# Attention layer of a graph network on one core: outputs' products and last channels' sums split by pair of chunks, and a new order of a step

## Chip, cores and metric

The kernel runs on one NeuronCore of a Trainium2 chip. The metric is the device time of one execution in microseconds. Several executions are timed, and one more is profiled; the profiled one has a time of its own.

## What is computed

Four graph layers work one after the other on 6250 nodes of 160 numbers (64 scalars and 32 vectors of three components) with 100,000 edges sorted by their target node. Each is followed by a residual sum and a layer norm. The change lies in the first, the attention layer. Cut to what matters:

```python
msg_s = (s_n @ Ws_src)[src] + (s_n @ Ws_dst)[dst]          # gathered per edge; vectors likewise
w1 = rbf @ W_rbf
m1_s, m1_v = _cg_tp(msg_s, msg_v, y0, y1, ...w1...)          # tensor product with the edge's direction
a = leaky(m1_s @ W_alpha); a = sum(a * alpha_dot)            # one score per head and edge
alpha = softmax of a over the edges of one target node
val_s, val_v = m1_s @ Ws_val, m1_v @ Wv_val, gated by sigmoid
m2_s, m2_v = _cg_tp(val_s, val_v, y0, y1, ...)
h = [m2_s @ Ws_vlin, m2_v @ Wv_vlin]
agg = segment_sum(alpha * h, dst)
out = node + [agg_s @ Wps, agg_v @ Wpv]
```

## The kernel before, in words

**Tiling.** Edges are cut into 784 chunks of 128. Four chunks (WC0) make a window, and 196 windows make the layer (`NST`, L1639). Class `Window0` (L1247) holds one window, and each of its methods is one stage of the work on it. Two chunks of a window make a pair `p`; each chunk sums into 16 target nodes of its own.

**Stages.** A window goes through these, in order of the data:
- `edges` (L1270, four calls) and `nodes` (L1276) gather rows from DRAM by an indirect DMA that GpSimd (POOL) issues, through the helper `gather` (L786, trace line L787).
- `masks`, `ends`, `weights` (TensorE, L1297 and L1302), `features` (DVE, L1308), `dots` (DVE, L1331), `dot` (GpSimd, L1335, two calls) and `product1` (DVE, four calls) make the first tensor product.
- For each chunk: `turn` (TensorE, three transposes, L1345), `turned` (ScalarE or ACT, L1350), `linear` (TensorE, three products, L1357), `tanh` (ACT, L1362), `directed` (DVE, L1372 to L1374).
- `crossed` (DVE, L1380), `joined` (GpSimd, L1386 and L1388), `gates`, `values` and `gated` make the values.
- `channels` (TensorE, L1415), `leak` and `leaky`, `scores` (TensorE, L1428), `largest` (DVE, L1437), `negated`, `exps`, `denominators` and `by_edge` (TensorE, L1466) make the attention weights. `weighted` (DVE, L1473) multiplies them with the edge's direction into the tile `py`.
- `sums` (TensorE, L1481, one call for each pair) sums values over the edges. `sums_z` (L1488, products at L1493) does it for the last 32 channels, 16 small products for all four chunks. `summed` and `summed_z` (ACT, L1486 and L1500) copy the sums out of PSUM.
- `outputs` (L1502, products at L1512) multiplies the sums with the outputs' weights: 40 small products, 20 for each pair, into one PSUM tile. `even` (ACT, L1517) and `odd` (DVE, L1521) take them out, and `write` sends the rows to DRAM by SyncE (SP).

Every float32 product is two rows of the trace (two passes), with as many weight loads.

**What sets the order.** Nothing is scheduled by the tool here: `edge_loop0` (L1601) runs under a manual schedule. A table written out by hand, `STEP0` (L1586), lists (lag, stage, argument). In step `s` the loop at L1661 goes down the table and calls each stage on window `s - lag`. So eight windows are in work at once (lags 0 to 7), and each engine's instructions stand in its queue in the order of this table. [...]

**Buffers.** PSUM tiles named `m` come from a ring of four banks (`bank`, L1337): each new one waits until the one four before it has been read. Fifteen are taken in a step. `wf` takes the other four banks. `py`, `a`, `az`, `q`, `th`, `xt` and the two `tp` tiles alternate between two buffers, `f` between five, `fw` between four.

**Every fourth step** (`k == 0`) the loads and the multiplication of the radial inputs take place: `radial_load` and `ends_load` on SP, `radial_turn` (GpSimd, L1570).

Behind the loop stands a slow path for edges that fit no window (L1668 on). It runs `todo_a` times and calls the same stages by name for one pair.

In the order before, TensorE's part of one step is: turns of two chunks, by_edge, ends, weights, turns of two chunks, scores, sums of pair 0, sums_z (16), linear of two chunks, sums of pair 1, linear of two chunks, channels, outputs (40). GpSimd's part is: dot 1, dot 2, nodes, edges 2, (radial_turn,) edges 0, edges 3, joined 0, edges 1, joined 1.

Of the kernel before, what the change touches and what calls it, by code (L numbers as in the profile page):

```python
# [18 lines left out]
P = 128  # L19
# [3 lines left out]
S, V = 64, 32  # L23
F = S + 3 * V
# [23 lines left out]
def kernel(ctx: ExitStack, tc: tile.TileContext, t: dict, out: bass.AP):  # L48
    nc = tc.nc
    vec, act, pe, pool = nc.vector, nc.scalar, nc.tensor, nc.gpsimd  # L50
# [151 lines left out]
    with tc.tile_pool(name="win", bufs=1) as sb, tc.tile_pool(name="winp", bufs=1, space=PSUM) as ps:  # L202
# [20 lines left out]
        for h in range(2):  # L223
            q = slice(h * WN, (h + 1) * WN)
# [7 lines left out]
        a = sb.tile([P, NCH], F32, name="a")  # L232
# [113 lines left out]
        for g, c in enumerate(ORDER0):  # L346
            q = slice(32 * g, 32 * g + 32)
# [4 lines left out]
        for h in range(2):  # L352
            q = slice(S * h, S * h + S)
# [893 lines left out]
    class Window0:  # L1247
# [12 lines left out]
        def __init__(self, w, sb, ps, n, k, radial, dst, gi, y, yc, ids, node_idx, rows, tps):  # L1260
            self.w, self.sb, self.ps, self.n, self.np = w, sb, ps, n, n // 2
            self.k, self.radial, self.dst = k, radial, dst
            self.gi, self.y, self.yc, self.ids, self.node_idx = gi, y, yc, ids, node_idx
            self.rows, self.tps = rows, tps
            self.t, self.z, self.pa = {}, {}, {}
            self.f = self.xt = self.th = self.q = self.val = self.a = None

            self.groups = [(g, c) for g, c in enumerate(ORDER0) if c < n]

# [215 lines left out]
                self.a = self.sb.tile([P, WC0, 4, S], F32, name="a", bufs=2)  # L1485
            act.copy(self.a[:, 2 * p : 2 * p + 2].rearrange("p c i m -> p (c i m)"), self.pa[p])  # L1486

        def sums_z(self):  # L1488

            self.pz = pa = self.bank()  # L1490
            for c in range(self.n):
                for i in range(4):
                    pe.matmul(  # L1493
                        pa[i * V : (i + 1) * V, c * S : (c + 1) * S], self.val[:, c, P:F], self.py[:, c, i, :], start=True, stop=True
                    )

        def summed_z(self):
# [1 line left out]
            self.az = self.sb.tile([P, WC0, S], F32, name="az", bufs=2)  # L1499
            act.copy(self.az[:, 0:n].rearrange("p c m -> p (c m)"), self.pz[:, 0 : n * S])  # L1500

        def outputs(self):  # L1502

            w = self.w["o"]
            self.po = po = self.bank()[:, 0:160].rearrange("p (a k) -> p a k", a=2)
            for p in range(self.np):
                for i in range(5):
                    for h in range(2):
                        for g in range(2):
                            q = slice(h * S + g * 32, h * S + g * 32 + 32)  # L1510
                            x = (self.a[:, 2 * p + h, i, :] if i < 4 else self.az[:, 2 * p + h, :])[:, g * 32 : g * 32 + 32]
                            pe.matmul(po[q, p, :], x, w[:, i, g, :], start=i == 0, stop=i == 4)  # L1512

        def even(self):

# [56 lines left out]
    class Ends:  # L1572
# [11 lines left out]


    STEP0 = [  # L1586
        (7, "summed", 1), (4, "linear", 1), (0, "radial_load"), (4, "tanh", 1), (4, "linear", 3), (1, "edges", 0),
        (5, "negated"), (3, "product1", 2), (4, "channels"), (1, "edges", 3), (4, "tanh", 3), (6, "denominators"),
        (4, "leak"), (4, "directed", 1), (5, "exps"), (7, "outputs"), (3, "turn", 3), (4, "directed", 3),
        (4, "leaky"), (5, "values"), (7, "even"), (3, "turn", 2), (4, "others"), (5, "by_edge"), (4, "crossed"),  # L1590
        (7, "odd"), (5, "gates"), (2, "ends"), (5, "weighted"), (4, "joined", 0), (3, "turned", 3),
        (3, "turned", 2), (2, "weights"), (3, "turn", 0), (3, "turned", 0), (3, "turn", 1), (2, "features"),
        (1, "edges", 1), (4, "scores"), (3, "bases"), (2, "dots"), (4, "largest"), (3, "turned", 1), (6, "sums", 0),
        (6, "summed", 0), (6, "sums_z"), (0, "ends_load"), (7, "write", 0), (3, "linear", 0), (5, "joined", 1),
        (3, "linear", 2), (6, "sums", 1), (2, "product1", 0), (2, "dot", 1), (2, "dot", 2), (1, "masks"),
        (3, "tanh", 0), (2, "product1", 1), (7, "write", 2), (7, "write", 1), (6, "summed_z"), (5, "gated"),
        (3, "tanh", 2), (0, "nodes"), (3, "directed", 0), (3, "directed", 2), (1, "edges", 2), (2, "product1", 3),
        (7, "write", 3), (0, "radial_turn"),
    ]

    def edge_loop0(w, res):  # L1601
        with tc.tile_pool(name="sb0", bufs=1) as sb, tc.tile_pool(name="ps0", bufs=1, space=PSUM) as ps:
# [37 lines left out]
            with tc.manual_schedule():  # L1640
                for s in range(NST + max(x[0] for x in STEP0)):
                    if s < NST:
# [10 lines left out]
                        q = slice(c0, c0 + WC0)  # L1653
# [13 lines left out]
        with ExitStack() as c2:  # L1667
            n_it = nc.values_load(todo_a[0:1, 0:1], min_val=0, max_val=NIT)  # L1668
            it = c2.enter_context(tc.For_i(0, n_it, 1))
            io = c2.enter_context(tc.tile_pool(name="late_0", bufs=1))  # L1670
            rows = ds(it * P, P)
            si = io.tile([P, CH], I32, name="si")
            nc.sync.dma_start(si, t["src_col"][rows, :])
            y5 = io.tile([P, CH, 5], F32, name="y5")
            nc.sync.dma_start(y5, t["ea5"][rows, :].rearrange("p (c i) -> p c i", i=5))

            y = io.tile([P, CH, 2, 6], F32, name="y")
            for h in range(2):
                vec.tensor_copy(y[:, :, h, 0:5], y5)
                vec.tensor_copy(y[:, :, h, 5:6], y5[:, :, 2:3])  # L1680
            at_ = io.tile([P, 1], F32, name="at0")
            vec.memset(at_, 0.0)
            c2.enter_context(tc.For_i(0, NP // (2 * WM0), 1))
            sb = c2.enter_context(tc.tile_pool(name="lsb0", bufs=1))
            ps = c2.enter_context(tc.tile_pool(name="lps0", bufs=1, space=PSUM))
            ids = sb.tile([P, 1], F32, name="ids")
            vec.tensor_scalar(ids, at_, slot0[:, 0:1], None, ALU.add)
            gi = sb.tile([P, 1], I32, name="gi")
            vec.tensor_copy(gi, ids)
            gh = sb.tile([P, 1], I32, name="gh")  # L1690
            vec.tensor_scalar(gh, at_, slot0[:, 1:2], None, ALU.add)
            vec.tensor_scalar(at_, at_, float(2 * WM0), None, ALU.add)
            tps, yb = rotating(sb, 1), with_ones(sb, 1, 1)
            flat = tabs[0][0][0].rearrange("i n w -> (i n) w")
            for c in range(CH):
                e = t["es16T"][:, ds(it * (CH * P) + c * P, P)].rearrange("i (c p) -> i c p", p=P)
                yrow = y_rows[ds(it * CH + c, 1), :].rearrange("(o c) p -> o c p", o=1)
                radial = Radial(sb, yb, {g: (e, yrow) for g, k in enumerate(ORDER0) if k < 2}, 1)
                dst = late0[ds(it * CH + c, 1), :].rearrange("(o c) p -> o c p", o=1)
                x = Window0(  # L1700
                    w, sb, ps, 2, 0, radial, Ends(sb, [dst, dst], 1), [si[:, c : c + 1]] * 2, y[:, c, :, 0:4],
                    y[:, c, :, 1:6], ids, gi, None, tps,
                )
                old = sb.tile([P, HW], F32, name="old")
                gather(old, flat, gh)
                for name in (
                    "edges 0", "edges 1", "nodes", "radial_load", "radial_turn", "ends_load", "masks", "others", "ends",
                    "weights", "features", "dots", "dot 1", "dot 2", "product1 0", "product1 1", "product1 2", "product1 3",
                    "turn 0", "turned 0", "linear 0", "tanh 0", "directed 0", "turn 1", "turned 1", "linear 1", "tanh 1",
                    "directed 1", "crossed", "joined 0", "joined 1", "gates", "values", "gated", "channels", "leak", "leaky",  # L1710
                    "scores", "largest", "negated", "exps", "denominators", "by_edge", "weighted", "sums 0", "summed 0",
                    "sums_z", "summed_z", "outputs", "even", "odd",
                ):
                    name, *arg = name.split()
                    arg = [old] if name in ("largest", "exps", "odd") else [int(k) for k in arg]
                    getattr(x, name)(*arg)
                pool.indirect_dma_start(
                    out=flat,
                    out_offset=bass.IndirectOffsetOnAxis(ap=gh, axis=0),
                    in_=x.row[:, 0, :],  # L1720
                    in_offset=None,
                    compute_op=ALU.bypass,
                )
# [36 lines left out]
    with ExitStack() as c0:  # L1760
        wp = c0.enter_context(tc.tile_pool(name="w0", bufs=1))
        with tc.tile_pool(name="nodes0", bufs=2) as sb, tc.tile_pool(name="nodes0p", bufs=2, space=PSUM) as ps:
            w = {
                "gamma_s": load_rows(wp, t["L0_gnn_gamma_s"], S, "gamma_s"),
                "beta_s": load_rows(wp, t["L0_gnn_beta_s"], S, "beta_s"),
                "s": [load(wp, t["L0_gnn_Ws_src"], S, S, "ws_src"), load(wp, t["L0_gnn_Ws_dst"], S, S, "ws_dst")],
                "v": [load_diag(wp, t["L0_gnn_Wv_src"], "wv_src"), load_diag(wp, t["L0_gnn_Wv_dst"], "wv_dst")],
            }
# [24 lines left out]
            for k in range(3):  # L1793
                q = slice(k * V, (k + 1) * V)
# [306 lines left out]
```

## Time and profile before

| | |
|---|---|
| time, median of 3 executions | 8291.0 us (8269.68 to 8301.09) |
| profiled execution, its own time | 8173.18 us |
| its span | 8170.2 us |
| attention layer in it (L1357's first to L1512's last product) | 361 to 2764 us |
| busy over the span | PE 6802.2, DVE 4949.3, POOL 4420.3, ACT 3575.2 us |
| outputs' products in the layer, L1512 | 12544 with `a`, 3136 with `az`; mean 236 ns each, overlapping |
| sums of the last channels, L1493 | 6272, median 219 ns, overlapping |
| gathers of edges' rows, L787 | 2352 in all layers, median 949 ns on GpSimd |

PE is TensorE's products and PEld its weight loads; the ends of products are modelled, and products overlap. "issue" as a releaser means that the engine waited for nothing that the profile shows. In lines of groups: line, engine, operation, names out<-in, shapes, count, then busy time and mean duration in ns, then idle time just before and what ended it. In lines of a timeline: start in us, duration in us, engine, line, operation, names, count, and in brackets the idle time before.

### The profile page before, as it was taken

Reading aid. Unit: us, or ns where it says so; the run is one execution under the profiler, and the core shown is the slowest. Engines: PE = TensorE matmul, PEld = TensorE weight load, DVE = VectorE, ACT = ScalarE, POOL = GpSimd, SP = SyncE. Lnnn points to the kernel's source line nnn. Section 1 sums busy time; section 2 is a strip of 40 time slices with the busy share of each in tenths; the row PEclk is TensorE's granted clock in tenths of the full one; section 3 lists DMA queues with packets and bytes.
Section 4 is the critical chain, followed back from the end, with each engine's and each line's share of the span. In section 5 each row is a group of like instructions: output and inputs, shape, how many; then the busy total and the mean of one; then the engine's idle time right before and its main releaser. Section 6 shows DMA issues by size and latency. Waiting matters only on the chain. (4 is left out here: it accounts for less than half of the span.)

```text
span 8170.2 us, 172707 instructions
## 1 busy us (share of the span) xinstructions
PE 6802.2 (83%) x60984; PEld 5281.2 (65%) x60984; DVE 4949.3 (61%) x12477; ACT 3575.2 (44%) x10875; POOL 4420.3 (54%) x4283
## 2 busy tenths in 40 slices
PE   1899999999899799999999997666667677777777
PEld 1677777777777569999999994444444454444446
DVE  5477777777777657777777775333333454444446
ACT  0254444455445445555555555333333332222224
POOL 0256555555555217777777771655555225555550
PEclk9999999999999759999999995788888788888888
DMA  3233333333222235656565554222222343333335
GB/s 133 84 99 101 99 98 98 101 100 97 56 57 58 70 108 98 103 98 102 98 102 98 102 81 148 64 65 65 65 65 66 115 135 84 82 82 83 81 84 216
DMA packets 669597, 763.72 MB, mean 93 GB/s; under 512 B 197530, under 2 KB 531515, under 8 KB 666907
## 3 DMA queue, kind: packets, MB, share of 16 engines
q0 software_dynamic: 239904, 294.05, 20.8%
q1 hardware_dynamic: 427642, 449.66, 17.8%
q8 instruction: 494, 8.09, 0.4%
q10 hardware_dynamic: 1152, 8.60, 0.3%
q14 instruction: 405, 3.31, 0.1%
HBM read 505.36 MB, written 246.53 MB: 92 GB/s over the span
## 5 line engine op out<-in xcount | busy, mean ns | idle before, releaser
L787 POOL DMA_INDIRECT f<-feat,r_src x2352 | 2301.6, 979 | 1713.2 <-issue 623.2
L1146 POOL DMA_INDIRECT tab<-o,scat x784 | 1346.2, 1717 | 437.2 <-ACT o L1145 312.1
L922 PE MATMUL pa<-pr,oy 128*128 128x321 f32 (+1 forms) x3136 | 1172.2, 513 | 14.8 <-ACT o L934 8.1
L931 ACT COPY o<-pa 32x96 f32<-32x96 f32 (+4 forms) x2358 | 550.7, 244 | 1229.2 <-issue 432.6
L872 PE MATMUL ww<-w,hid 64*128 64x192 f32 (+1 forms) x2088 | 357.5, 474 | 733.8 <-DVE pr L914 315.0
L922 PEld LDWEIGHTS pa<-pr,oy 128*128 128x128 f32 x3136 | 655.0, 213 | 420.5 <-issue 286.5
L1132 PE MATMUL pt<-same,tp 128*128 128x128 f32 x6272 | 895.5, 286 | 7.0 <-DVE tp L775 4.0
L872 PEld LDWEIGHTS ww<-w,hid 64*128 64x128 f32 x2088 | 245.3, 253 | 879.2 <-ACT o L934 342.8
L1132 PEld LDWEIGHTS pt<-same,tp 128*128 128x128 f32 x6272 | 764.3, 192 | 24.2 <-PE pf L1116 16.3
L1134 ACT COPY xt<-pt 128x512 f32<-128x512 f32 x784 | 459.6, 586 | 525.2 <-PE pt L1132 517.2
L1357 PE MATMUL m<-w_m,xt 128*128 128x128 f32 x4704 | 610.1, 280 | 8.4 <-ACT az L1500 3.8
L911 DVE TENSOR_TENSOR pr<-f,ww 128x384 f32<-128x384 f32 x131 | 72.7, 555 | 894.2 <-ACT wy L876 697.4
L1143 PE MATMUL po<-ov,xt 128*128 128x32 f32 x4704 | 611.6, 267 | 0.0
L1357 PEld LDWEIGHTS m<-w_m,xt 128*128 128x128 f32 x4704 | 571.3, 192 | 38.2 <-ACT az L1500 4.6
L1143 PEld LDWEIGHTS po<-ov,xt 128*128 128x128 f32 x4704 | 588.3, 192 | 0.0
L907 DVE TENSOR_TENSOR pr<-f,ww 128x384 f32<-128x384 f32 x131 | 72.5, 553 | 799.6 <-remote 356.6
L1512 PE MATMUL m<-w_o,a 128*32 128x80 f32 x12544 | 392.2, 236 | 193.4 <-issue 191.8
L1512 PEld LDWEIGHTS m<-w_o,a 128*32 128x32 f32 x12544 | 289.9, 110 | 328.9 <-issue 289.9
L876 ACT ACTIVATE wy<-ww,r_y 128x96 f32<-128x96 f32 x784 | 196.1, 348 | 592.8 <-issue 571.2
L1362 ACT ACTIVATE th<-m 128x96 f32<-128x96 f32 x784 | 196.6, 251 | 543.3 <-PE m L1357 231.4
L1372 DVE TENSOR_TENSOR q<-m,yc 128x192 f32<-128x192 f32 x784 | 276.8, 353 | 233.9 <-ACT th L1362 175.3
L1350 ACT COPY xt<-m 128x384 f32<-128x384 f32 x784 | 334.4, 484 | 191.4 <-PE m L1345 185.5
(353 smaller groups left out, 14449.8 us busy)
## 6 DMA issues: line engine op xcount, KB each, us to landing
tab<-zeros SPq DMA_DIRECT2D x131, 512.0 KB
nodes<-in_src_row_dram SPq DMA_DIRECT2D x98, 512.0 KB
f<-feat,r_src POOLq DMA_INDIRECT x2352
tb<-tab SPq DMA_DIRECT2D x24, 1280.0 KB
dn<-in_dst_row_dram SPq DMA_DIRECT2D x98, 256.0 KB
e<-in_ef64T_dram SPq DMA_DIRECT2D x196, 128.0 KB
dn<-in_dst_row_dram SPq DMA_DIRECT2D x196, 128.0 KB
e<-in_ef64T_dram SPq DMA_DIRECT2D x261, 96.0 KB
```

The source lines that it names most:

```text
L787: pool.indirect_dma_start(out=o, out_offset=None, in_=table, in_offset=bass.IndirectOffsetOnAxis(ap=idx, axis=0),)
L872: pe.matmul(self.ww[:, q, 0:wn], self.hid[k, c * P : (c + 1) * P], m, start=True, stop=True)
L922: pe.matmul(pa[:, 0:m], self.oy[:, q, :], self.pr[:, q, 0:m], start=c == 0, stop=c == self.ns[h] - 1)
L931: act.copy(o[q, at : at + e], pa[q, b0 * V : b0 * V + e])
L1132: pe.matmul(pt[:, k, :], self.tp[:, c, lo : lo + P], self.same[:, c, :], start=True, stop=True)
L1134: act.copy(self.xt, pt)
L1143: pe.matmul(po[:, 96 + i * V : 96 + (i + 1) * V], xt[:, 1 + i, :], w["ov"], start=True, stop=True)
L1146: pool.indirect_dma_start(out=self.tables[c % len(self.tables)], out_offset=bass.IndirectOffsetOnAxis(ap=self.scat[:, c : c + 1], axis=0), ...
L1350: act.copy(self.xt[:, :, c, :], self.t[c][:, 0 : 3 * P].rearrange("p (k e) -> p k e", k=3))
L1357: pe.matmul(z[:, k, :], self.xt[:, k, c, :], self.w["m"][:, k, :], start=True, stop=True)
L1372: vec.tensor_mul(q[:, 0:2], x[:, 1:3], turns)
L1512: pe.matmul(po[q, p, :], x, w[:, i, g, :], start=i == 0, stop=i == 4)
```

## The change

`sums_z` and `outputs` get an argument, the pair `p`, and do only this pair's share: 8 of the 16 small sums, 20 of the 40 products. The first call of a window takes the PSUM tile, the second writes the other half of it. `STEP0` is replaced by a new table: it calls `sums_z` and `outputs` twice and puts all stages in a new order with new lags, up to 10. The slow path calls each of the two once, with pair 0, which is all that it has.

```diff
-        def sums_z(self):
-
-            self.pz = pa = self.bank()
-            for c in range(self.n):
+        def sums_z(self, p):
+
+            if self.pz is None:
+                self.pz = self.bank()
+            for c in range(2 * p, 2 * p + 2):
                 for i in range(4):
                     pe.matmul(
-                        pa[i * V : (i + 1) * V, c * S : (c + 1) * S], self.val[:, c, P:F], self.py[:, c, i, :], start=True, stop=True
+                        self.pz[i * V : (i + 1) * V, c * S : (c + 1) * S], self.val[:, c, P:F], self.py[:, c, i, :], start=True, stop=True
                     )
...
-        def outputs(self):
+        def outputs(self, p):
 
             w = self.w["o"]
-            self.po = po = self.bank()[:, 0:160].rearrange("p (a k) -> p a k", a=2)
-            for p in range(self.np):
-                for i in range(5):
...
+            if self.po is None:
+                self.po = self.bank()[:, 0:160].rearrange("p (a k) -> p a k", a=2)
+            for i in range(5):
+                for h in range(2):
+                    for g in range(2):
+                        q = slice(h * S + g * 32, h * S + g * 32 + 32)
+                        x = (self.a[:, 2 * p + h, i, :] if i < 4 else self.az[:, 2 * p + h, :])[:, g * 32 : g * 32 + 32]
+                        pe.matmul(self.po[q, p, :], x, w[:, i, g, :], start=i == 0, stop=i == 4)
...
+        (5, "crossed"), (3, "radial_turn"), (3, "weights"), (9, "even"), (9, "odd"), (4, "turn", 2), (5, "leak"),
+        (7, "summed", 1), (5, "leaky"), (6, "gated"), (4, "turn", 0), (9, "write", 0), (4, "turned", 2),
+        (10, "write", 1), (1, "edges", 1), (4, "turn", 3), (4, "turned", 0), (3, "features"), (7, "sums_z", 1),
+        (0, "nodes"), (7, "sums_z", 0), (4, "turned", 3), (6, "exps"), (5, "scores"), (3, "product1", 0),
+        (2, "masks"), (10, "write", 3), (5, "largest"), (4, "turn", 1), (3, "dots"), (7, "summed_z"),
+        (8, "sums", 0), (6, "by_edge"), (5, "gates"), (4, "linear", 3), (6, "weighted"), (4, "turned", 1),
+        (8, "summed", 0), (4, "linear", 1), (4, "tanh", 3), (4, "tanh", 1), (4, "linear", 0), (3, "bases"),
+        (0, "edges", 3), (4, "directed", 3), (5, "joined", 0), (4, "linear", 2), (5, "joined", 1), (3, "dot", 1),
+        (5, "negated"), (4, "directed", 1), (3, "product1", 1), (0, "radial_load"), (9, "write", 2), (4, "tanh", 0),
+        (8, "outputs", 1), (4, "directed", 0), (6, "sums", 1), (1, "edges", 2), (3, "dot", 2), (5, "values"),
+        (8, "outputs", 0), (3, "product1", 3), (4, "channels"), (4, "tanh", 2), (3, "product1", 2), (2, "ends"),
+        (0, "ends_load"), (4, "directed", 2), (6, "denominators"), (0, "edges", 0), (4, "others"),
```

TensorE's part of one step now is: weights, turns of three chunks, sums_z 1 and 0 (8 and 8), scores, the fourth turn, sums of pair 0, by_edge, linear of all four chunks, outputs 1 (20), sums of pair 1, outputs 0 (20), channels, ends. GpSimd's part is: edges 1, nodes, edges 3, joined 0, joined 1, dot 1, edges 2, dot 2, edges 0. After every fourth step's edges 0 follows radial_turn. The lines behind `Window0.sums_z` move down by one in the changed kernel (the products of the outputs are L1513 there).

More of the change, by code (lines that the diff above doesn't have):

```diff
@@ L1265, in __init__ @@
             self.t, self.z, self.pa = {}, {}, {}
-            self.f = self.xt = self.th = self.q = self.val = self.a = None
+            self.f = self.xt = self.th = self.q = self.val = self.a = self.pz = self.po = None
             self.groups = [(g, c) for g, c in enumerate(ORDER0) if c < n]
@@ L1500, in summed_z @@
             act.copy(self.az[:, 0:n].rearrange("p c m -> p (c m)"), self.pz[:, 0 : n * S])
-        def outputs(self):
+        def outputs(self, p):
             w = self.w["o"]
-            self.po = po = self.bank()[:, 0:160].rearrange("p (a k) -> p a k", a=2)
-            for p in range(self.np):
-                for i in range(5):
[L1508 to L1512, printed above, removed]
+            if self.po is None:
[6 more added lines that the diff above has]
+                        pe.matmul(self.po[q, p, :], x, w[:, i, g, :], start=i == 0, stop=i == 4)
         def even(self):
@@ L1586 @@
     STEP0 = [
[L1587 to L1596, printed above, removed]
@@ L1597 @@
-        (3, "tanh", 2), (0, "nodes"), (3, "directed", 0), (3, "directed", 2), (1, "edges", 2), (2, "product1", 3),
-        (7, "write", 3), (0, "radial_turn"),
+        (5, "crossed"), (3, "radial_turn"), (3, "weights"), (9, "even"), (9, "odd"), (4, "turn", 2), (5, "leak"),
+        (7, "summed", 1), (5, "leaky"), (6, "gated"), (4, "turn", 0), (9, "write", 0), (4, "turned", 2),
+        (10, "write", 1), (1, "edges", 1), (4, "turn", 3), (4, "turned", 0), (3, "features"), (7, "sums_z", 1),
+        (0, "nodes"), (7, "sums_z", 0), (4, "turned", 3), (6, "exps"), (5, "scores"), (3, "product1", 0),
@@ L1711, in edge_loop0 @@
                     "scores", "largest", "negated", "exps", "denominators", "by_edge", "weighted", "sums 0", "summed 0",
-                    "sums_z", "summed_z", "outputs", "even", "odd",
+                    "sums_z 0", "summed_z", "outputs 0", "even", "odd",
                 ):
```

## Prediction

> **What bounds the kernel now.** I read the slices first, then the busy table by stretches, the costliest groups, and the timeline of single steps. The change touches the attention layer only, some 361 to 2766 us of a span of 8170.2 us (first product of L1357 to last of L1512, rounded). There TensorE never rests:
>
> ```profile
> PE   1899999999899799999999997666667677777777
> ...
> POOL 0256555555555217777777771655555225555550
> ```
>
> The stretches say how near the others are (columns: stretch, length, then busy time of PE, PEld, DVE, ACT, POOL, clock, DMA share, GB/s):
>
> ```profile
> 1200.00:1400.00 200.00, 182.57 (x2953) 148.01 (x2954) 157.59 (x512) 99.65 (x314) 119.23 (x153) 1.00 0.38 99
> ```
>
> A step (four chunks of edges, 196 steps) takes 12.26 us, the mean distance of the bursts of L1512 in the timeline. So per step PE is busy 11.2 us and DVE 9.7. PE is the bound, but part of its time is no work. The groups show where:
>
> ```profile
> L787 POOL DMA_INDIRECT f<-feat,r_src x2352 | 2301.6, 979 | 1713.2 <-issue 623.2
> ...
> L1512 PE MATMUL m<-w_o,a 128*32 128x80 f32 x12544 | 392.2, 236 | 193.4 <-issue 191.8
> ```
>
> 192 us of PE idle before the outputs' products end in "issue": no semaphore is waited for. One burst (80 products and 80 weight loads) in the timeline:
>
> ```profile
> 1019.51 0.39 PE L1415 MATMUL m<-xt,w_alpha 128*64 128x256 f32 x2
> 1019.83 0.74 PE L1512 MATMUL m<-w_o,a 128*32 128x80 f32 x26
> 1021.59 0.32 PE L1512 MATMUL m<-w_o,a 128*32 128x80 f32 x4 [1.02 <-issue]
> ```
>
> 26 products start within 0.5 us, then nothing for 1.25 us from start to start. The mean burst, first to last start, is 3.05 us. What GpSimd does meanwhile:
>
> ```profile
> 1014.69 0.99 POOL L1335 TENSOR_TENSOR d<-d 128x128 f32<-128x128 f32 x2 [3.42 <-DVE d L1331]
> 1015.91 0.97 POOL L787 DMA_INDIRECT fw<-feat,win0G  x1 [0.23 <-issue]
> 1017.18 0.95 POOL L787 DMA_INDIRECT f<-feat,r_src  x1 [0.30 <-issue]
> 1018.44 0.95 POOL L787 DMA_INDIRECT f<-feat,r_src  x1 [0.30 <-issue]
> 1019.69 0.95 POOL L787 DMA_INDIRECT f<-feat,r_src  x1 [0.30 <-issue]
> ```
>
> Four gathers in a row, started once "dots" (L1331) is done. PE resumes 1.9 us after the last one starts; where the row starts 0.3 us later against the burst, the stall also ends 0.3 us later. Without gathers there is no stall:
>
> ```profile
> 2178.99 0.76 PE L1512 MATMUL m<-w_o,a 128*32 128x80 f32 x32
> 2179.57 0.32 PE L1512 MATMUL m<-w_o,az 128*32 128x80 f32 x8
> 2179.70 0.74 PE L1512 MATMUL m<-w_o,a 128*32 128x80 f32 x32
> 2180.26 0.32 PE L1512 MATMUL m<-w_o,az 128*32 128x80 f32 x8
> ```
>
> ```profile
> 2180.43 0.72 POOL L1386 TENSOR_TENSOR q<-q 128x256 f32<-128x256 f32 x1 [6.85 <-DVE q L1380]
> ```
>
> Here GpSimd waits 6.85 us, and 80 products start in 1.36 us (17 ns each). The last six bursts of the layer, when nothing is left to gather, are like it. So **the stall is a meeting of a dense burst with gathers**. Counting loads and products from 0.3 us after a row's first gather to the stall gives about 46 + 13.8 per us (fit over 188 bursts): 62 with one gather before it (45 bursts), 102 with four (137). [...] a row of gathers lets through about 14 per us. Products of L1357 (17 instructions per us) barely feel that; a burst of 110 per us does.
>
> [...]
>
> **The change part by part.**
> *Work.* The 16 sums of the last channels become 2 x 8 and the 40 products become 2 x 20 (each is two passes in the trace, so 32 and 80 rows, and as many weight loads). Count and duration are unchanged: 0. The two calls of sums_z have nothing of PE between them, so that part changes nothing by itself.
> *Banks.* Both PSUM banks are held across two calls. The outputs' bank is reused four allocations later, by "turn 0". PE does channels 0.58, ends 0.38, weights 0.49, a turn 0.36 = 1.8 us between; "even" (0.33) and "odd" (0.30) need some 0.75 if ACT and DVE are ready. Cost 0; if DVE is late (its work is 9.7 us a step), up to 0.5 us, kept for the range. The new waits on ACT and DVE at both output calls are met 0.6 us or more earlier by this count (directed 3 on DVE is the latest). If not, sums 1, channels and all PE work queued behind wait, and with channels the next step's leak on ACT and leaky on DVE.
> *PE without stall.* From the timeline's group lengths: channels 0.58, ends 0.38, weights 0.49, four turns 1.42, sums_z 0.58, scores 0.43, sums 0.96 + 0.87, by_edge 0.31, linears 2.87, outputs 2 x 0.73 = 10.35 us. This is the floor for either order.
> *Gathers.* GpSimd's queue is now dots' sums (dot 1), gather, dot 2, then edges 0, edges 1, nodes, edges 3, then the joins. Dot 1 still waits for dots, which DVE does right after "largest", which waits for scores. So dots ends at about the end of outputs 0 + (0.58 + 0.38 + 0.49 + 3 x 0.36 + 0.58 + 0.43) + 0.1 + 0.42 + 0.56 = 4.6 us; dot 1 starts at 4.7 (before, last product of L1512 to dot 1: 3.7). From dot 1: edges 2 at 0.7, dot 2 at 1.65, edges 0 at 2.3, and at 1.26 each edges 1, nodes, edges 3 at 6.1 (before, dot 1 to its last gather: 5.0). By 1.9 us later the row lets go: 8.0.
> *Bursts in that row.* PE needs from outputs 0: 3.52 + turn 0.36 + sums 0.96 + by_edge 0.31 + linears 2.87 = 8.0, so outputs 1 starts 3.3 after dot 1, 1.0 after edges 0 starts. Between 2.6 and 8.0 the row lets through 46 + 13.8 x 5.4 = 120 instructions. Outputs 1, sums 1 and outputs 0 and the rest of the linears need 12 + 80 + 8 + 80 = 180. So the 60 left go after 8.0, in 0.5 us. The step is 4.7 + 8.0 + 0.5 = 13.2 us, against 11.8 of the undisturbed step now (bursts at 1019.83 and 1031.63): **+1.4 us**. Bounds: if the row lets 26 per us through (twice the fit) the outputs end before it does and the step is 12 or less; if it ends 3 us after the last gather, as some long stalls did, 14.3.
> *Every fourth step.* radial_turn (1.29 us on GpSimd) now splits this row behind edges 0. The gap lets most of both bursts through; I get 11.9 to 13.5 against some 12.9 now, and take -0.2.
> *The rest of STEP0.* ACT (6.1 us a step) and SP have room, and moved loads and writes stay a step or more ahead of their readers: 0 (if a write is late, "even" waits; none is seen). The longest lag grows from 7 to 10, but outputs only from 7 to 8: about 8 us at the end.
> *Sum.* (3/4 x 1.4 - 1/4 x 0.2) x 196 = +196, +8 = +204 us. The profiled execution (8173.18, span 8170.2) becomes 8377. The median shown lies 118 above it, so 8291 + 204 = **8495**.
>
> **The rivals.**
> *A: faster, the short bursts fit.* Each burst is 80 instructions, [...] and the stall (3.05 - 1.36 = 1.7 us a step) goes. DVE at 9.7 us then is late at times; with 0.5 us for that, 10.35 + 0.5 = 10.85, -1.4 x 196 + 8 = -266; with a third of the stall left, about -215: 8076. It decides from 26 instructions per us, or if the row of gathers falls elsewhere. For it: 80 is near the 74 to 84 that a burst with one gather just before it got through. Against: outputs 0 comes 1.6 us later, with the row still running.
> *B: no difference.* The step is set by dots, row of gathers, burst, both before and after; if the splits and the longer row balance (PE stalls once, 1.7 us), 8291 + 8 = about 8300.
> *Forecast: slower,* the row of gathers now starts with the first burst and covers the second.
>
> **How the numbers follow.** A measurement tells about 0.5% (41 us). Forecast 0.60, its own range 8350 to 8640 (13.8 per us up to some 20, tail 1.5 to 3 us). A 0.30 (7990 to 8200), B 0.10. For 8 in 10 the range runs from 8050, inside A, to 8630.
>
> **What would show it.** Right: the step from 12.26 to about 13.2, "issue" idle before L1513 in outputs 1's end or outputs 0, ending about 1.9 us after the fourth gather of a row; dots to outputs as computed. A: "issue" before L1513 under 60 us and steps under 11.2. Wrong in another way: PE idle on DVE or ACT at turns (banks), or gathers not in a row. The other three layers should not move.

## The result and the profile after

The changed kernel takes 8849.9 us (median of four executions, 8822.0 to 8856.0), the kernel before 8285.5 (8269.7 to 8301.1) beside it: **1.0675 times as long, interval 1.0643 to 1.0706**. 8495 was forecast, with a range up to 8630. The direction was right; the loss of 564 us is 2.8 times the 204 forecast.

The profiled execution of the changed kernel took 8853.3 us (span 8850.2). Its slices, and behind them the granted clock of PE in the slices of before:

```profile
PE   2888888888888887999999999766666676777777
...
POOL 0344444444444440377777777255555505555551
PEclk9988889898899886799999999578888887888888
```

```profile
PEclk9999999999999759999999995788888788888888
```

In the attention layer (slices 2 to 16 of the changed kernel) PE fell from 9 to 8 tenths, GpSimd from 5 to 4, and the granted clock of PE is 8 or 9 tenths in most slices. The layer as a stretch, from the first to the last outputs' product, first the kernel before, then the changed one (length, busy PE, PEld, DVE, ACT, POOL, then granted clock, DMA share, GB/s):

```profile
400.00:2764.00 2364.00, 2152.98 (x34984) 1743.84 (x34985) 1845.71 (x5969) 1181.74 (x3671) 1375.90 (x1763) 0.99 0.33 85
```

```profile
409.00:3381.00 2972.00, 2574.77 (x34902) 1967.85 (x34901) 1842.70 (x5943) 1202.56 (x3655) 1354.12 (x1749) 0.88 0.26 67
```

The same products keep PE busy 422 us longer, and PE is idle 397 us in place of 211. DVE, ACT and GpSimd do what they did before. Two effects, then: idle time, and **slower products**. Only the first was in the forecast. The two groups of the outputs' products, with PE's idle time just before them at the end of each line, and behind them the second group in the kernel before (the first stands in the prediction):

```profile
L1513 PE MATMUL m<-w_o,a 128*32 128x80 f32 x12544 | 400.3, 257 | 123.5 <-issue 121.9
...
L1513 PE MATMUL m<-w_o,az 128*32 128x80 f32 x3136 | 223.8, 259 | 157.7 <-issue 153.7 <-DVE tp L1322 3.1 <-DVE q L1374 0.5
```

```profile
L1512 PE MATMUL m<-w_o,az 128*32 128x80 f32 x3136 | 162.1, 235 | 10.8 <-issue 10.0
```

Together 276 us end in "issue"; before it was 202. The 74 us more are a small part of 564 us. GpSimd's row in one step of the changed kernel:

```profile
1512.62 0.46 POOL L1335 TENSOR_TENSOR d<-d 128x128 f32<-128x128 f32 x1 [5.28 <-DVE d L1331]
1513.23 0.97 POOL L787 DMA_INDIRECT f<-feat,r_src  x1
1514.22 0.46 POOL L1335 TENSOR_TENSOR d<-d 128x128 f32<-128x128 f32 x1
1514.84 0.96 POOL L787 DMA_INDIRECT f<-feat,r_src  x1 [0.16 <-issue]
1516.11 0.95 POOL L787 DMA_INDIRECT f<-feat,r_src  x1 [0.30 <-issue]
1517.36 0.95 POOL L787 DMA_INDIRECT fw<-feat,win0G  x1 [0.30 <-issue]
1518.61 0.95 POOL L787 DMA_INDIRECT f<-feat,r_src  x1 [0.30 <-issue]
```

and PE in the same step, from the last of the linears on:

```profile
1515.55 0.76 PE L1513 MATMUL m<-w_o,a 128*32 128x80 f32 x32
1516.13 0.35 PE L1513 MATMUL m<-w_o,az 128*32 128x80 f32 x7
1516.95 0.24 PE L1513 MATMUL m<-w_o,az 128*32 128x80 f32 x1 [0.47 <-issue]
1517.12 1.16 PE L1481 MATMUL m<-py,val 128*128 128x256 f32 x4
1518.21 0.33 PE L1513 MATMUL m<-w_o,a 128*32 128x80 f32 x2
1519.12 0.32 PE L1513 MATMUL m<-w_o,a 128*32 128x80 f32 x2 [0.58 <-issue]
1520.54 0.91 PE L1513 MATMUL m<-w_o,a 128*32 128x80 f32 x26 [1.10 <-issue]
...
1521.78 1.12 PE L1415 MATMUL m<-xt,w_alpha 128*64 128x256 f32 x4
1522.83 0.92 PE L1297 MATMUL wf<-fw,on 16*128 16x160 f32 x8
```

GpSimd goes through its queue in the table's order: edges 2, which needs nothing of dots, starts at 1513.23, behind dot 1, which waited 5.28 us for it. The row lies where it was computed: edges 2 at 0.6 after dot 1, dot 2 at 1.6, the last gather at 6.0. Outputs 1 start 2.9 after dot 1 (3.3 forecast), trickle, and PE is released at 1520.54, 1.93 us after the last gather. The last two lines show the surprise: L1415 and L1297 take 1.12 and 0.92 us where in the next step they take 0.65 and 0.55 (at 1536.71 and 1537.29). **PE runs at half clock** after the stall:

```profile
1520.00:1525.00 5.00, 4.46 (x62) 2.97 (x62) 1.66 (x4) 1.22 (x4) 0.72 (x2) 0.66 0.10 22
1525.00:1530.00 5.00, 5.00 (x67) 4.49 (x66) 4.11 (x13) 3.83 (x12) 1.89 (x3) 1.00 0.09 24
```

In the layer the trace's clock record holds 686 us at half clock in 142 spells; before, 24 us in 5.

### The profile page after: what moved, and what is told of

It reads as the page before. It is cut to its first block, busy times and chain, and to the rows that moved or that the text cites. A ratio compares the mean times of both kernels' runs of the same rounds, so it can differ in the third digit from the quotient of the medians.

```text
span 8850.2 us, 172164 instructions
## 1 busy us (share of the span) xinstructions
PE 7230.9 (82%) x60984; PEld 5513.3 (62%) x60984; DVE 4955.3 (56%) x12477; ACT 3599.5 (41%) x10875; POOL 4416.1 (50%) x4283
## 5 line engine op out<-in xcount | busy, mean ns | idle before, releaser
L1335 POOL TENSOR_TENSOR d<-d 128x128 f32<-128x128 f32 x392 | 180.6, 461 | 1349.7 <-DVE d L1331 1345.3
L1357 PE MATMUL m<-w_m,xt 128*128 128x128 f32 x4704 | 560.4, 276 | 1.9 <-issue 1.9
L1481 PE MATMUL m<-py,val 128*128 128x256 f32 x1568 | 490.0, 425 | 82.1 <-issue 78.7
L1357 PEld LDWEIGHTS m<-w_m,xt 128*128 128x128 f32 x4704 | 543.7, 193 | 2.5 <-issue 2.3
L1518 ACT ACTIVATE row<-m,own 128x80 f32<-128x80 f32 x196 | 64.4, 329 | 1127.6 <-PE m L1513 868.2
L1513 PE MATMUL m<-w_o,a 128*32 128x80 f32 x12544 | 400.3, 257 | 123.5 <-issue 121.9
L1522 DVE SCALAR_TENSOR_TENSOR row<-m,own,row 128x80 f32<-128x80 f32 x196 | 59.1, 301 | 777.3 <-ACT row L1518 776.9
```

What stands on the lines that cost most here:

```text
L1357: pe.matmul(z[:, k, :], self.xt[:, k, c, :], self.w["m"][:, k, :], start=True, stop=True)
L1481: pe.matmul(pa[:, h * 256 : (h + 1) * 256], self.val[:, c, 0:P], py, start=True, stop=True)
L1513: pe.matmul(self.po[q, p, :], x, w[:, i, g, :], start=i == 0, stop=i == 4)
```

## The experiments

The theory after the result, T1 ("Theory 1" in the first expectations): gathers in a row hold up PE where it has a dense burst, and the stalls make the clock drop. The kernel before measured 8273, 8182 and 8250 us in the three sets of runs, so the ratio to the kernel before of the same set counts. "Half clock" and "idle" below are of the layer, from the first to the last outputs' product of the profiled execution.

**1 and 2. No gathers in the windows, both orders.**

```diff
-            gather(self.f[:, c, :], feat[0][:, :], self.gi[c])
+            nc.sync.dma_start(self.f[:, c, :], feat[0][c * P : (c + 1) * P, :])
...
-            gather(self.fw, feat[1][:, :], self.node_idx)
+            nc.sync.dma_start(self.fw, feat[1][0:P, :])
```

> The kernel before with the same replacement; the same part is left out. Theory 1: the 1.7 us stall of each step goes, step 10.4 to 10.9 us, time 7900 to 8030. Theory 3: about 8285, stall as before. Theory 2 says nothing of it.

Measured 7897.2 us, ratio 0.954 (0.952 to 0.956): as T1 has it. Idle falls from 211 to 25 us; no burst stalls.

> The changed kernel with the layer's five gathers a window replaced by plain copies of as many rows, issued by SyncE. Left out: the rows are fixed ones, not those of the edges, so the output isn't the reference's. Theory 1 (GpSimd's issuing of gathers holds back TensorE's instructions, and the long stall halves TensorE's clock): no stall in either burst, full clock, step 10.6 to 11 us, time 7900 to 8050. Theory 2 (the split itself or the bank held across two calls costs): stays 8700 to 8900. Theory 3 (the moved bytes, not GpSimd, hold TensorE back): stays 8600 to 8900.

Measured 8185.0, ratio 0.989 (0.987 to 0.991), above what T1 expected. The typical step (median 10.6 us, no stall) is what T1 said; but about every fourth step (46 of 195) takes over 12 us, half of those over 17. There `largest` on DVE waits for an earlier window's row to land in DRAM:

```profile
DVE s L1443 <- DMA tab<-row: 176.8, 44, 5.3
```

The changed kernel itself has no such wait (there "largest", L1437, waits 124.7 us for PE in the layer and never for a DMA). The copies stand on SyncE's queue, which also sends those rows, so I put the excess down to this edit; that is argued, not tested apart. The layer takes 263 us more than 195 typical steps, and these steps hold nearly all of it. Even so, without gathers the new order is not slower than the kernel before.

**3. New order, outputs in one burst.** Of the changed kernel, `(8, "outputs", 1)` goes to right before `(8, "outputs", 0)`.

> The changed kernel with outputs 1 moved down to stand right before outputs 0: one burst of 40 products again, all else in the new order. Theory 1: the end of the row of gathers sets the end of the burst, as with two; 8700 to 8880. Theory 2 (the split costs): back under 8450.

Measured 8705.2, ratio 1.051 (1.049 to 1.054), just within T1's numbers. Half clock 423 us. Most of the loss stays with one burst, but joining gives back 1.6 of the 6.75%: in this order the early place of the first half does cost something.

**4. Split methods in the old order.** The halves stand next to each other.

> The old table with the new methods: sums_z 0 and 1 next to each other, outputs 0 and 1 next to each other, where the whole calls stood. Theory 1: the same as before, 8265 to 8305. Theory 2: slower than before by over 1%.

Measured 8272.2, ratio 1.000 (0.999 to 1.001). In the old order, with the halves next to each other, the split costs nothing; the loss comes with the new order. Its profiled execution (8273.1 us span) is also a better base than that of before, which was 110 us quicker than its median:

```profile
396.00:2814.00 2418.00, 2176.51 (x34979) 1762.09 (x34969) 1838.45 (x5966) 1176.32 (x3671) 1373.90 (x1764) 0.98 0.32 84
```

**5. The changed kernel with GpSimd's queue alone reordered.** Edges 0 goes before dot 2, the joins behind dot 2.

```diff
-        (0, "edges", 3), (4, "directed", 3), (5, "joined", 0), (4, "linear", 2), (5, "joined", 1), (3, "dot", 1),
+        (0, "edges", 3), (4, "directed", 3), (4, "linear", 2), (3, "dot", 1),
...
-        (8, "outputs", 1), (4, "directed", 0), (6, "sums", 1), (1, "edges", 2), (3, "dot", 2), (5, "values"),
+        (8, "outputs", 1), (4, "directed", 0), (6, "sums", 1), (1, "edges", 2), (0, "edges", 0), (3, "dot", 2), (5, "values"),
...
-        (0, "ends_load"), (4, "directed", 2), (6, "denominators"), (0, "edges", 0), (4, "others"),
+        (0, "ends_load"), (4, "directed", 2), (6, "denominators"), (5, "joined", 0), (5, "joined", 1), (4, "others"),
```

> The changed kernel with GpSimd's queue alone put in another order: dot 1, edges 2, edges 0, dot 2, joined 0, joined 1, then edges 1, nodes, edges 3. TensorE's order and the split stay. Theory 1: the sums stand where the bursts are, so outputs 1 meets one gather's tail and outputs 0 at most the start of the next row; most of the stall and all of the halved clock go, step 11 to 12 us, time 8050 to 8250. Theory 2 (split or bank): 8750 to 8900.

Measured 8473.4, ratio 1.035 (1.034 to 1.037): a miss. The bursts are nearly free of stalls, as meant (PE's idle time before L1513 that ends in "issue" is under 5.8 us between 1000 and 1400 us, 35.4 in the changed kernel), and the row of edges 1, nodes, edges 3 now meets ends, weights and turns, which are sparse. It costs there too. Part of it goes another way than in the bursts. Timeline of that stretch, three engines:

```profile
1208.60 0.32 PE L1513 MATMUL m<-w_o,az 128*32 128x80 f32 x8
...
1211.06 0.94 POOL L787 DMA_INDIRECT f<-feat,r_src  x1 [0.30 <-issue]
...
1212.76 0.33 ACT L1518 ACTIVATE row<-m,own 128x80 f32<-128x80 f32 x1 [5.86 <-PE m L1345]
...
1213.12 0.30 DVE L1522 SCALAR_TENSOR_TENSOR row<-m,own,row 128x80 f32<-128x80 f32 x1 [3.89 <-ACT row L1518]
...
1213.48 1.54 PE L1345 MATMUL m<-ident,tp 128*128 128x128 f32 x6 [1.73 <-DVE row L1522]
```

The last output product ends at 1208.9. "Even" (L1518) needs nothing else of PE, ACT has been idle for 5.86 us, and yet it starts at 1212.76, 1.7 us after the last gather's start. So **PE's finished work reaches ACT late**, and because outputs hold a bank, PE's next turn waits for "odd". Taken over the trace, for "even" where ACT stood idle before the burst's end: it starts 0.05 us after that end in the changed kernel where no gather has started in the 2 us before the end (150 times), 3.3 us after it where one has (46 times). In this kernel the second case occurs 174 times, mean 2.9 us. Without gathers (run 2): 0.07 us, every time. The lateness is on PE's side: in all of these 46 and 174 cases ACT starts within 0.024 us of the update of the semaphore that the last product sends, and it is this update that comes late. As the ends of products are modelled, the trace does not tell a late signal from a late end.

PE's waits for "odd" are only 47 us of this layer. The larger part of the loss is products that trickle while gathers run and count as busy: PE is busy 277 us longer than in run 4 with the same work. By the count of work explained behind run 10, half clock explains 84 of them; at full clock, busy time exceeds work by 292 us within 2 us of a gather's start and by 29 elsewhere (run 4: 89 and 32).

**6. One of the five gathers taken out of the changed kernel.** Only the nodes become a plain copy on SyncE.

> The changed kernel with one of the row's four gathers (nodes) replaced by a plain copy of fixed rows on SyncE; left out: the right rows of the target nodes. Theory 1: the row ends 1.26 us earlier, so the stall is as much shorter (-250 us in all)[...], which gives back some of the 340 us of halved clock: 8400 to 8620. A theory in which each gather costs TensorE the same: one fifth of the loss against the plain copies, about -170: 8680. Theory 2: 8850.

Measured 8273.5, ratio 1.011 (1.010 to 1.013), 8378 on the scale of 8285. One gather of five takes away 5.6 of the 6.75%. "Each gather costs the same" is out, and T1's numbers were too high. Half clock falls from 686 to 78 us, and PE's idle time from 397 to 193: the clock, not the stall alone, makes the effect so uneven.

**7. A better place for one gather in the kernel before.** Edges 3 moves behind joined 0.

```diff
-        (5, "negated"), (3, "product1", 2), (4, "channels"), (1, "edges", 3), (4, "tanh", 3), (6, "denominators"),
+        (5, "negated"), (3, "product1", 2), (4, "channels"), (4, "tanh", 3), (6, "denominators"),
...
-        (1, "edges", 1), (4, "scores"),
+        (1, "edges", 3), (1, "edges", 1), (4, "scores"),
```

> The kernel before with edges 3 moved behind joined 0, next to edges 1: the row ahead of the burst has three gathers in place of four, and ends 1.26 us earlier. Theory 1: the stall shrinks from 1.7 to about 0.5 us a step, 8050 to 8120. If only the number of gathers in a step counts: 8285.

Measured 8006.5, **ratio 0.979 (0.977 to 0.980), quicker than both kernels**. The row is three gathers, a wait for DVE, then two:

```profile
1512.01 1.01 POOL L787 DMA_INDIRECT fw<-feat,win0G  x1 [0.23 <-issue]
1513.34 0.95 POOL L787 DMA_INDIRECT f<-feat,r_src  x1 [0.31 <-issue]
...
1515.74 0.97 POOL L787 DMA_INDIRECT f<-feat,r_src  x1 [0.16 <-issue]
1517.55 0.73 POOL L1386 TENSOR_TENSOR q<-q 128x256 f32<-128x256 f32 x1 [0.83 <-DVE q L1380]
1518.42 0.98 POOL L787 DMA_INDIRECT f<-feat,r_src  x1
1519.70 0.95 POOL L787 DMA_INDIRECT f<-feat,r_src  x1 [0.30 <-issue]
```

(The gap between the second and third is the radial multiplication of every fourth step.) Idle in the layer 73 us, half clock 7.

**8. Plain copies again, this time issued by GpSimd.** As run 1, with `pool.dma_start`.

> The kernel before, its order unchanged; the gathers of edges and nodes in the attention layer's fixed windows are replaced by plain copies of fixed rows, and this time GpSimd issues them, at the same places of its queue (so the layer computes on other rows). T5 (what holds PE up is GpSimd's work of making an indirect gather, 0.95 us each): a plain copy takes GpSimd much less, the burst of 80 products runs through in 1.4 us and the time is as with copies by SyncE, 0.95 to 0.97 of the kernel before. T6 (any DMA issued by GpSimd, or its traffic, holds PE up): the stall of about 1.7 us in the burst stays, 0.99 to 1.01. A copy by GpSimd that costs it as long as a gather would give T6's time for T5's reason; its duration in the trace tells.

Measured 7856.7, ratio 0.952 (0.950 to 0.953). T5: neither DMAs issued by GpSimd nor their traffic hold PE up; what an indirect gather has beyond a plain copy does. GpSimd's row, then the same time on PE:

```profile
1510.76 0.55 POOL L1285 DMA_DIRECT2D fw<-feat  x1
1511.31 1.59 POOL L1277 DMA_DIRECT2D f<-feat  x3
```

```profile
1200.00:1400.00 200.00, 200.00 (x3438) 167.47 (x3437) 182.33 (x599) 119.58 (x365) 96.79 (x178) 1.00 0.41 121
```

A copy takes GpSimd 0.54 us, a gather 0.95. PE is busy without a gap. (Whether it is the indexing, the scattered addresses or the longer work of a gather that matters, this run does not separate.) 121 GB/s pass meanwhile, more than the 99 of the kernel before, and GpSimd's own queue moves 4737 packets of the same three sizes in these 200 us, against 3936 there. The step is 10.42 us, the same at the 10th, 50th and 90th percentile: this is the floor, 10.35 forecast.

**9. Two gathers moved in the kernel before.** Edges 0 and edges 3 go behind joined 0.

> The kernel before with two gathers, edges 0 and edges 3, moved behind joined 0 on GpSimd's queue, next to edges 1 (edges 3 alone gave 0.979 of the kernel before, with 0.38 us of stall left in the burst and a step of 11.4 us). T1 (the burst meets too long a row): the row with the burst has two gathers left, 0.38 us of stall goes, three gathers in a row now lie on sparse products: step 10.9 to 11.4 us, 0.966 to 0.982. Rival: joined 1 and with it dot 1 come 1.3 us later, or the row of three holds back PE's signals as in the kernel with GpSimd's queue moved: 0.985 to 1.01.

Measured 8178.2, ratio 0.990 (0.989 to 0.992): the rival's numbers. The outputs' burst is free (1.8 us of idle time before it end in "issue" between 420 and 2700 us, 198.7 in the kernel before), but the row of three now meets sums_z, 32 small products in 0.65 us, and the turns' consumers:

```profile
PE m L1493 <- issue: 120.1, 242, 1.5
PE m L1493 <- ACT xt L1350: 50.4, 26, 2.6
```

"Turned" (L1350) on ACT, where ACT stood idle before (200 of 784 times), starts 1.2 us after the turn's end in the mean (0.04 without gathers, but 0.9 in run 7 too, the quickest with gathers: lateness alone does not decide).

**10. The changed kernel with its bursts out of the row.** GpSimd's queue is left alone; both outputs move to behind the fourth turn, at lag 9, with even and odd behind them (`write` 0 to lag 10; the sums get one buffer ring for each pair, one deep for pair 0 and three for pair 1).

```diff
-        (2, "masks"), (10, "write", 3), (5, "largest"), (4, "turn", 1), (3, "dots"), (7, "summed_z"),
+        (2, "masks"), (10, "write", 3), (5, "largest"), (4, "turn", 1), (3, "dots"), (9, "outputs", 1), (9, "outputs", 0), (9, "even"), (9, "odd"), (7, "summed_z"),
```

> The changed kernel with GpSimd's queue untouched; on PE's queue outputs 1 and outputs 0 are moved out of the row of gathers, to behind the fourth turn and dots (lag 9), even and odd right behind them, and the sums get a buffer for each pair. The row of gathers then meets sums, linears, channels, ends and weights, which are sparse. T1 (bursts meeting the row make the stalls, and the stalls make the clock drop): both stalls and nearly all low clock go, step 10.6 to 11.4 us, 0.95 to 0.985 of the kernel before. T4 (what else the new order does, its held banks or signals that come late, costs as much): step 12.5 us or more, low clock stays above 200 us, 1.01 to 1.05.

Measured 8660.3, ratio 1.050 (1.048 to 1.052): T4, and **T1 in its narrow form falls**. The stall in the bursts is nearly gone (0.04 us of idle a step before outputs' products, against 1.4 in the changed kernel), and PE waits elsewhere:

```profile
PE wf L1297 <- DVE tp L1322: 157.3, 102, 2.9
PE m L1345 <- ACT a L1487: 136.7, 81, 2.8
PE m L1466 <- ACT az L1502: 93.2, 101, 2.3
```

All three are waits for ACT or DVE to empty a buffer. I put them down to PE's late signals, which ACT's queue has to wait for; how much of them the new places of even and odd cost by themselves is not shown. "Even" again starts 1.4 us after the burst's end in the mean where a gather is near (115 times), 0.07 where none is (81). Idle 480 us, half clock 440.

**What goes ahead of a drop of the clock.** Half-clock spells last 3.41 us or a multiple of it in the records (in the changed kernel's layer 88 of 3.41, 49 of 6.83 and 5 of 10.24 us), so I compared PE's idle time in the 3.41 us before each. Before: all five spells follow more than 1.8 us of idle, and no stretch followed by full clock has more than 1.42. Run 10: 93% of 81 spells follow more than 1.7 us, 0.6% of the stretches followed by full clock do, none over 1.81. The changed kernel: median 1.72, and the longest without a drop 1.73; but a quarter of its 110 spells (from 430 to 2700 us) follow less than 1.25. Run 5 speaks against idle time as the measure: its 60 spells follow 0.61 us in the median, and only one follows more than 1.7.

"Busy" hides products that trickle (the 292 us of run 5). So count work instead: each product by its mean distance to the next one in run 8, where nothing stalls (18 ns for an outputs' product with `a`, 120 for one of L1357). Over the eleven traces that have spells, 97% of the 486 drops from full to half clock follow less than 1.6 us of such work in 3.41 us, and 4% of the 6595 stretches that stay at full clock do; between 1.2 and 1.6 both are seen. Run 5 fits too (median 1.29), and so does the odd quarter of the changed kernel (median 1.30). The kernel before has less than 1.6 us in 30 of 660 full-clock stretches, the changed one in 193 of 649. This is what goes ahead of the drops; no run changed the amount of work by itself.

| run | ratio | layer, us | idle | half clock |
|---|---|---|---|---|
| 8 GpSimd's plain copies | 0.952 | 2015 | 0 | 0 |
| 1 SyncE's plain copies | 0.954 | 2059 | 25 | 10 |
| 7 edges 3 moved | 0.979 | 2193 | 73 | 7 |
| 2 changed, SyncE's plain copies | 0.989 | 2330 | 204 | 195 |
| 9 two moved | 0.990 | 2322 | 202 | 41 |
| 4 old order, split | 1.000 | 2418 | 241 | 82 |
| 6 changed, nodes plain | 1.011 | 2421 | 193 | 78 |
| 5 changed, GpSimd's queue | 1.035 | 2636 | 182 | 256 |
| 10 changed, bursts moved | 1.050 | 2776 | 480 | 440 |
| 3 new order, one burst | 1.051 | 2825 | 426 | 423 |
| changed kernel | 1.068 | 2972 | 397 | 686 |

## Why the prediction was wrong in size

**The sum, term by term**, against run 4, whose layer takes 2418 us (the changed kernel 2972, +554; all behind the layer 5459 and 5469).
- *Clock: forecast 0, about +287.* The step that failed is "PE without stall ... 10.35 us. This is the floor for either order": it holds for full clock alone (run 8: 10.42), and the forecast has no term for a step that stalls longer and runs on at half clock. PE is busy 653 us of the time at half clock, 79 in run 4; half of the difference is 287. Counted as work at run 8's distances, these products are worth 333 us and 42, which gives a loss of 284 more than in run 4. The numbers were in the trace of before: five spells at half clock, each behind more idle time (over 1.8 us in 3.41) than any stretch that kept full clock (1.42 at most). In the changed kernel PE was idle for about half of the 3.41 us ahead of a spell (median 1.72), in pieces of at most 1.1 us in the step shown.
- *Stall: forecast +196, about +268.* Idle +156 (397 against 241), and of the 398 us of added busy time the 112 that the clock doesn't explain, which are products trickling through the row: at full clock, busy time exceeds the work done by 247 us within 2 us of a gather's start and not at all elsewhere (run 4: 89 and 32). The mis-sized figure is what a row lets through. The forecast took 46 + 13.8 per us, or 120 loads and products from 0.3 us after edges 0 to the release; in 139 rows of four of the changed kernel it is 90 in the mean, in 5.5 us. In the step shown about 80 start in the first 1.5 us behind edges 0 and only 19 in the 4.2 us from there to the release. So more was left to do behind it.
- *Every fourth step: forecast -0.2 us, it is +1.0.* From one dot 1 to the next, these steps take 14.4 us (13.4 in run 4), the others 15.7 (12.2; +3.5 where +1.4 was forecast), clock and stall together. Shorter than the others, as argued, but the radial multiplication doesn't save them.
- *Work, split, rest of the table: forecast 0.* Run 4 confirms the split where the halves stand together. *Drain: +8*, not measured apart.

**Right:** the place and length of the row, its release 1.9 us after the last gather, the start of outputs 1 (2.9 for 3.3), that both bursts stall, that banks are harmless in this order (PE's waits for ACT and DVE at turns come to 0.2 us in the layer), and the other layers (10 us). The step of 12.26 us is 12.1 over all 195 distances of the bursts; the sum does not rest on it.

**Incomplete:** "Products of L1357 barely feel that; a burst of 110 per us does." Runs 5, 9 and 10 show that other parts pay as well: sparse products trickle too, and PE's signal came 3.8 us late in the step of run 5 shown. In the kernel before, "even" starts 1.0 us after the burst's end in the mean where a gather is near and ACT stood idle (50 times; 0.05 where none is, 14 times), but PE waits for ACT and DVE only 4.4 us in the whole layer, so there the lateness lay where nobody waited.

**Rivals:** A (faster, the short bursts fit) falls: the burst of outputs 0 lies in the row in full. B (no difference) falls with it.

Still open: by what path a gather holds up PE's instructions and its signals; whether little work by itself is what halves the clock; how far the stall and the clock feed each other (a slow step shifts the next row).

## What to carry to other kernels

Put indirect gathers on GpSimd in short rows, with waits between, and look in the trace for what TensorE and its readers do until its release (1.9 us after the last gather's start here); moving one of five was worth 2% here and the whole new order lost 7%. When a change lengthens TensorE's stalls, price the clock as well: ask whether a step has more stretches with little work than before (here under 1.6 us in 3.41, the length of the shortest spell), since here the whole loss came to twice the stall's, 554 us to 268. Count work, not busy time: products that trickle look busy (292 us in run 5). A place that is good for one engine's burst may be bad for the readers of another stage (two gathers moved gave 0.990, one 0.979), so a moved row needs every stage under it named.

## What the runs showed of the hardware that was not expected

- Indirect gathers (0.95 us each on GpSimd) delay both TensorE's instructions and the semaphore updates of its products. A row of four lets some 100 loads and products through in the kernel before and 90 in the changed one, in 5.4 and 5.5 us to the release. ScalarE starts 0.05 us after the last product's modelled end without gathers near, 3.3 with them. With plain copies by GpSimd, 0.54 us each at the same places, TensorE is busy for all of the 200 us from 1200 (run 8); with SyncE's, ScalarE starts after 0.07 us (run 2).
- Half clock lasts 3.41 us or a multiple, and 97% of the drops to it (486 in eleven traces) follow 3.41 us in which TensorE did less than 1.6 us of work by its full-clock distances; it need not have been idle in one piece, and by the busy time it was idle only 0.61 us of the 3.41 in the median of run 5.
- The outputs' products, four to different columns at a time, start 17 ns apart in the mean as long as nothing gathers (80 in 1.4 us, run 8).
